# Last token block's products moved to the end, state loads moved behind the third up group, one normalization and one projection moved

## The chip, the cores and the metric

The kernel runs on one core of a Trainium2 chip. The time is the device time of one execution in microseconds, the median of several runs; before the change it is 433.28 us (three runs, 433.25 to 434.26). A profiled execution gives the trace from which the lines below come.

## What is computed

A gated linear-state layer followed by a feed-forward layer with binarized weights, each with a residual and a layer norm, on an input of 2 sequences of 4096 tokens with 256 features:

```python
u = x @ W_in + b_in
g = sigmoid(x @ W_gate + b_gate)
h_t = tanh(h_prev @ A + u_t @ Bm)
y_t = h_t @ C.T + u_t @ D.T
y_t = g_t * y_t + (1.0 - g_t) * x_t
x = layernorm(x + (ys @ W_out + b_out + x))

bw = mean(abs(w), axis=1) * sign(w)
h = gelu(einsum('bsd,hd->bsh', x, bw1) + b1)
out = einsum('bsh,dh->bsd', h, bw2) + b2
x = layernorm(x + out)
```

The state has 64 entries, the hidden layer of the feed-forward part 1024.

## The kernel before

**Scan and chunks.** Each sequence is cut into 64 segments of 64 steps that are scanned side by side. The scan runs 40 warm-up steps and then 64 steps; one step is a product on TensorE (PE) with 128 columns (`steps`, L165) and a tanh on ScalarE (ACT, L170). The tokens of four steps form a chunk: 512 tokens, four blocks (`TB`) of 128. There are 16 chunks. At the end a count (`compare`, `count`, L172 to L186) checks that the warm-up has converged; if not, a slow path (L892 and after) computes all again.

**A chunk's stages**, as methods of `Chunk`: `load_u` and `load_h` copy the chunk's inputs and states of the scan into the tile hu (L355, L359, on SyncE's queue, SP); `load_x`, `load_n` load x; `gate` (L322) with a tanh; `mix` (L383, PE, then L390 on VectorE, DVE); `mix_end` (L395, L398, DVE); `project` (L408, PE, two halves, then the sum L419 on DVE); `stats1` (L264 to L274: block statistics, their merge and a sum on DVE, the reciprocal root on GpSimd, POOL); `shift` (L279, DVE) and `norm` (L287, four ACT instructions of 128x256). Then the normalized chunk is transposed: chunks 0, 1 and 15 by `turn` on PE (L442) with copies to a high part (L450, ACT) and a low part (L452, DVE); the others by `blocks`, a DVE transpose (L461) and sixteen small copies on SP's queue (L467), split by `split_hi` (L475, ACT) and `split_lo` (L479, DVE).

The feed-forward part goes in four groups of 256 hidden features. `up(g)` makes two products tiles ps_h (L498), a gelu for each (L508, ACT) and a copy to the rounded high part hhi (L517, ACT); `low(g)` the low part hlo (L524, DVE); `down(g)` adds 16 products per half (L540) into ps_o: for each of two feature blocks and each token block one product with the high and one with the low part. After group 3 come `scale` (L556, DVE), `add` (L562), statistics and `store` (normalization and an output DMA, L577).

**Order.** It is written out by hand for all engines: each engine and queue runs its instructions in the program's order. The main loop (L792 to L869) goes over c = 0 to 14; iteration c runs up, low and down of chunk c, the end of chunk c-1 (down groups 2 and 3), the transposition of chunk c+1, and mix, projection and statistics of chunk c+2, and loads for chunk c+3 and beyond. `step()` puts in one scan step where the next is ready; `do(c + 3, "load")` puts in as many steps as chunk c+3's states need and then issues both state loads. In iterations 10 and 11 one more `step()` stands ahead of the mix (L806). In iteration 0, `down` group 0 stands ahead of `project` of chunk 2. In iteration 14 the normalization of chunk 15 stands between up groups 0 and 1 of chunk 14.

**Buffers.** PSUM has these pools: p_s (one tile, the scan), p_m with one buffer of two banks under the tag "m" (ps_y of mix, ps_z of the projection, ps_t of the transposes, and ps_p at the end), p_1 with three single banks under the tag "h" (ps_h, ps_g and others), p_2 with one buffer of two banks (ps_o). The tiles h have two buffers, hhi and hlo three, x tiles "xt" eight.

**The end.** After the loop, chunk 15's groups are run; `down(0, True)` puts its four token blocks on four different banks, two of ps_o and two of ps_p. Then `down_end` (L594) runs the products of groups 2 and 3 block by block (`products`), scales each block, adds blocks 0 to 2 on POOL and block 3 on DVE, gathers statistics, and normalizes and stores each block: blocks 0 and 1 on ACT (which needs a shift from DVE), 2 and 3 on DVE.

## Time and profile before

| | us |
|---|---|
| median of three runs | 433.28 |
| the profiled execution | 433.4 |
| its span, first to last instruction | 431.6 |
| last product on PE ends | 423.4 |
| DVE busy | 337.0 |
| ACT busy | 282.3 |
| POOL busy | 165.2 |
| state loads L359: issue to landing, minimum, median, maximum | 2.2, 2.3, 7.3 |
| x loads L347: issue to landing, minimum, median, maximum | 3.3, 3.5, 3.6 |
| x loads L104: issue to landing, minimum, median, maximum | 3.2, 6.4, 9.5 |

All times in the text are microseconds from the start of the span. The page gives busy time per engine, and busy shares in 40 slices of the span. A product on PE is recorded with its whole passage through the array, so records of back-to-back products overlap: what a product costs is the distance between two starts, 0.115 for 256 columns of L540, 0.23 for 512 columns of L498. "PEld" is the load of the stationary operand. The chain of waits goes back from the last instruction, at each step to what released it; "issue" is time in which nothing that the profile shows was waited for. In the timeline, square brackets hold the idle time ahead of an instruction and its releaser.

### The profile page before, as it was taken

To read this page: it belongs to the slowest core of one execution; us is meant where nothing else is said; L and a number is where in the kernel's file an instruction comes from. 1 tells how busy PE (TensorE), PEld (TensorE's weight loads), DVE (VectorE), ACT (ScalarE), POOL (GpSimd) and SP (SyncE) were. 2 spreads that over 40 slices of the span, in tenths; PEclk is the share of its full clock that TensorE was granted. 3 is DMA by queue.
4 is the path that set the end of the run, shared out by engine and by line. 5 is a ranking of instruction groups with operands and counts; after the bars stand their busy time and mean duration, and the time that the engine had idled before them with its cause. 6 is when DMAs were issued, how large, how long until landed. Compare 5 with 4: busy or idle time off the path is not lost.

```text
span 431.6 us, 6781 instructions
## 1 busy us (share of the span) xinstructions
PE 421.7 (98%) x2390; PEld 342.8 (79%) x2390; DVE 337.0 (78%) x571; ACT 282.3 (65%) x469; POOL 165.2 (38%) x176
## 2 busy tenths in 40 slices
PE   8999999999999999999999999999999999999992
PEld 5576767788978888887978787979797888888982
DVE  0255477995979797979798888889797979789684
ACT  3353533386586867777676767676777685859881
POOL 1000013574155554344525453544443444415513
PEclk9999999999999999999999999999999999999997
DMA  8885555000252625162515242524242232311102
GB/s 285 296 286 203 159 159 171 1 2 0 47 174 45 225 45 176 41 219 49 177 40 184 81 140 75 194 72 145 75 127 87 59 115 59 111 37 50 49 2 103
DMA packets 31047, 49.24 MB, mean 114 GB/s; under 512 B 5281, under 2 KB 19873, under 8 KB 31009
## 3 DMA queue, kind: packets, MB, share of 16 engines
q1 hardware_dynamic: 30432, 48.39, 35.5%
q8 instruction: 21, 0.34, 0.3%
q10 hardware_dynamic: 576, 0.37, 0.3%
q14 instruction: 18, 0.14, 0.1%
HBM read 29.33 MB, written 8.39 MB: 87 GB/s over the span
## 4 chain that ended last, share of the span: by engine, by line
PE 89%; DVE 4%; SPq 2%; ACT 2%; DMA 1%; issue 0%; POOL 0%; POOLq 0%; ACTq 0%; DVEq 0%
PE ps_h L498 24%; PE ps_o L540 24%; PE ps_g L322 13%; PE ps_z L408 12%; PE ps_y L383 6%; PE ps_s L165 5%; PE ps_u L138 3%; SPq L467 2%; ACT xn L287 1%; DMA w_gate<-in_W_gate 1%; DVE hlo L524 1%; PE ps_t L442 1%; DMA xlo<-xb 0%; PE ps_p L540 0%; DVE d L395 0%
## 5 line engine op out<-in xcount | busy, mean ns | idle before, releaser
L540 PE MATMUL ps_o<-sg,hhi 128*128 128x256 f32 x496 | 120.6, 284 | 0.2 <-DVE o L556 0.2
L540 PE MATMUL ps_o<-sg,hlo 128*128 128x256 f32 x496 | 117.6, 278 | 0.1
L508 ACT ACTIVATE h<-ps_h,bias_c,al 128x512 f32<-128x512 f32 x128 | 95.3, 771 | 15.0 <-PE ps_h L498 10.8
L368 POOL TENSOR_TENSOR xn<-xn,bo_r 128x256 f32<-128x256 f32 x64 | 61.1, 987 | 102.2 <-DVE sg L204 61.3
L540 PEld LDWEIGHTS ps_o<-sg,hhi 128*128 128x128 f32 x496 | 93.4, 188 | 1.6 <-DVE o L556 0.6
L540 PEld LDWEIGHTS ps_o<-sg,hlo 128*128 128x128 f32 x496 | 93.4, 188 | 1.4 <-DVE hlo L524 0.3
L498 PE MATMUL ps_h<-xhi,sg 128*128 128x512 f32 x256 | 92.8, 444 | 0.1
L524 DVE TENSOR_TENSOR hlo<-h,hhi 128x1024 fp32r<-128x1024 f32 (+1 forms) x65 | 80.9, 1263 | 4.6 <-ACT hhi L517 4.6
L498 PE MATMUL ps_h<-xlo,sg 128*128 128x512 f32 x256 | 79.7, 393 | 0.0
L517 ACT CAST hhi<-h 128x1024 fp32r<-128x1024 f32 (+1 forms) x65 | 67.4, 1039 | 2.0
L322 PE MATMUL ps_g<-xt,w_gate 128*128 128x384 f32 (+3 forms) x212 | 66.2, 425 | 0.3 <-DMA w_gate<-in_W_gate 0.3
L274 POOL TENSOR_TENSOR rs_b<-rs_b,neg_half 128x4 f32<-128x4 f32 (+1 forms) x17 | 28.2, 1659 | 98.4 <-DVE rs_b L273 93.4
L498 PEld LDWEIGHTS ps_h<-xhi,sg 128*128 128x128 f32 x256 | 46.5, 189 | 18.7 <-issue 9.6
L170 ACT ACTIVATE st<-ps_s 64x128 f32<-64x128 f32 x103 | 27.5, 267 | 45.9 <-PE ps_s L165 45.5
L498 PEld LDWEIGHTS ps_h<-xlo,sg 128*128 128x128 f32 x256 | 48.1, 188 | 10.9
L368 POOL TENSOR_TENSOR xn<-xn,b_r 128x256 f32<-128x256 f32 x64 | 55.8, 903 | 1.1 <-PE ps_t L442 1.1
L408 PE MATMUL ps_z<-w_out,tg 128*128 128x256 f32 x224 | 50.6, 379 | 0.0
L165 PEld LDWEIGHTS ps_s<-st,wab 128*128 128x128 f32 x208 | 35.6, 189 | 18.2 <-ACT st L170 9.3
L408 PEld LDWEIGHTS ps_z<-w_out,tg 128*128 128x128 f32 x224 | 41.4, 190 | 5.1
L475 ACT CAST xhi<-xlo 128x1024 fp32r<-128x1024 f32 x13 | 13.7, 1051 | 42.1 <-DVE nm_b L279 20.3
L165 PE MATMUL ps_s<-st,wab 128*128 128x128 f32 x208 | 40.4, 276 | 0.0
L322 PEld LDWEIGHTS ps_g<-xt,w_gate 128*128 128x128 f32 x212 | 33.1, 191 | 7.4 <-issue 5.3
(79 smaller groups left out, 485.2 us busy)
## 6 DMA issues: line engine op xcount, KB each, us to landing
xt<-in_xT SPq DMA_DIRECT2D x31, 512.0 KB, 4.3
xn<-in_x SPq DMA_DIRECT2D x16, 512.0 KB, 3.3
out_y<-xn SPq DMA_DIRECT2D x15, 512.0 KB, 2.6
xlo<-xb SPq DMA_DIRECT2D x208, 32.0 KB, 1.9
hu<-st SPq DMA_DIRECT2D x32, 128.0 KB, 2.3
w1t<-in_w1T SPq DMA_DIRECT2D x2, 512.0 KB, 5.5
w1n<-in_w SPq DMA_DIRECT2D x2, 512.0 KB, 6.7
w2t<-in_w2T SPq DMA_DIRECT2D x2, 512.0 KB, 6.9
```

Of the source, the lines that this page charges most:

```text
L165: nc.tensor.matmul(p_h, ab, st[:, j].rearrange("p b k -> p (b k)"), start=True, stop=True)
L170: nc.scalar.activation(h_of[:, j + 1].rearrange("p b k -> p (b k)"), p_h[TOP, :], AF.Tanh)
L274: nc.gpsimd.tensor_tensor(rs, rs, neg_half[:, cut], ALU.pow)
L322: nc.tensor.matmul(ps[:, cut], w_gate[:, m, k, :], xt_[:, k, cut], start=k == 0 and i == 0, stop=k == KD - 1, skip_group_check=True,)
L368: nc.gpsimd.tensor_tensor(r[:, i, :], r[:, i, :], row, ALU.add)
L383: nc.tensor.matmul(ps[:, m, :], cd[:, bass.ts(m, P)], self.hu, start=True, stop=True)
L408: nc.tensor.matmul(self.ps_z[:, i, :], self.y[:, k, bass.ts(i, P)], w_out[:, k, :], start=k == 0, stop=k == KD - 1,)
L498: nc.tensor.matmul(ps, sg1[:, k, bass.ts(j, P)], part[:, k, :], start=n == 0, stop=n == 2 * KD - 1,)
L508: nc.scalar.activation(to, ps.rearrange("p (a i c) -> p a i c", a=P // 32, c=32) if self.far else ps, AF.Gelu, bias=b1_c[:, j : j + 1], sc ...
L517: nc.scalar.copy(hi[:, part, :], h[:, part, :])
L524: nc.vector.tensor_sub(lo[:, i, :], h[:, i, :], hi[:, i, :].bitcast(FP))
L540: nc.tensor.matmul(ps[:, i, :], part[:, j % 2, bass.ts(tb, P)], sg2[:, j, :], start=j == 0 and part is self.h[j // 2][0] and first, stop=j ...
```

## The change

- The end: block 3 of chunk 15 gets no products in down groups 0 and 1; all its sixteen come last. Blocks 2 and 3 get banks of their own from the pool p_1 (`own_bank`). The high and low part of group 3 take buffers of the x tiles. Within `down_end` products run first over group 2 for three blocks, then over group 3 block by block; the statistics of blocks 0 and 1 stand ahead of block 3's scale on DVE; their shift moves from DVE to three small ACT instructions (`shift_alone`); block 3 is stored ahead of block 2, and the queues of the two are swapped.
- `load_u` stays where both state loads were, `load_h` moves behind up group 2 and its step; with it the rule that fills in missing steps. The two extra steps of iterations 10 and 11 are gone; in the order that comes out, two more steps run in iteration 12, behind its up groups 1 and 2.
- In iteration 14 the normalization of chunk 15 moves between the two gelus of up group 1.
- In iteration 0 the projection of chunk 2 moves ahead of down group 0.

```diff
+        def shift_alone(self, blocks):
+
+            cut = slice(blocks[0], blocks[-1] + 1)
+            self.sh = sm.tile([P, TB], FP, tag="nm", name=f"nm_{self.name}_{blocks[0]}")
+            nc.scalar.activation(self.sh[:, cut], self.mv[:, cut, 0], AF.Identity, scale=-1.0)
+            for i in blocks:
+                sh = self.sh[:, i : i + 1]
+                nc.scalar.activation(sh, sh, AF.Identity, scale=self.rs[:, i : i + 1])
...
-            hi = wk.tile([P, 2, N], FR, tag="hhi", name=f"hhi{nm}", bufs=3)
+            if apart:
+                hi = xp.tile([P, 2, N], FR, tag="xt", name=f"hhi{nm}", bufs=XTB)
+            else:
+                hi = wk.tile([P, 2, N], FR, tag="hhi", name=f"hhi{nm}", bufs=3)
...
-            lo = wk.tile([P, 2, N], FR, tag="hlo", name=f"hlo{self.nm}_{g}", bufs=3)
+            if apart:
+                lo = xp.tile([P, 2, N], FR, tag="xt", name=f"hlo{self.nm}_{g}", bufs=XTB)
+            else:
+                lo = wk.tile([P, 2, N], FR, tag="hlo", name=f"hlo{self.nm}_{g}", bufs=3)
...
-                self.banks = [((self.ps_o, other)[tb % 2], tb // 2 * 2, True) for tb in range(TB)]
+                self.banks = [(self.ps_o, 0, True), (other, 0, True), self.own_bank(2)]
+
+        def own_bank(self, tb):
+            ps = p_1.tile([P, N], FP, tag="h", name=f"ps_q{self.nm}_{tb}")
+            return ps.rearrange("p (i d) -> p i d", d=DM), 0, True
...
-                for tb in range(TB):
+                for tb in range(len(self.banks)):
                     self.down_part(2 * g + i, tb)
...
-            for tb in range(2):
-                products(tb)
-                add(tb)
-            st2.gather([0])
-            products(2)
-            add(2)
-            st2.gather([1])
-            st2.merge([0, 1])
-            st2.root([0, 1])
-            products(3)
-            add(3)
-            st2.shift([0, 1])
-            store(0, nc.scalar)
-            store(1, nc.scalar)
-            st2.gather([2, 3])
-            st2.merge([2, 3])
-            st2.root([2, 3])
-            store(2, nc.vector)
-            store(3, nc.vector)
+            for tb in range(last):
+                products(tb, range(KH // 2, KH - 2))
+            for tb in range(last):
+                products(tb, range(KH - 2, KH))
+                self.scale(range(tb, tb + 1))
+                add(tb, nc.gpsimd)
+            products(last, range(KH))
+            early, late = [0, 1], [2, last]
+            st2.gather(early)
+            st2.merge(early)
+            st2.root(early)
+            self.scale([last])
+            add(last, nc.vector)
+            st2.gather(late)
+            st2.merge(late)
+            st2.root(late)
+            st2.shift_alone(early)
+            store(0, nc.scalar, nc.sync)
+            store(1, nc.scalar, nc.scalar)
+            store(last, nc.vector, nc.sync)
+            store(2, nc.vector, nc.scalar)
...
-        if what == "load":
+        if what == "load_h":
             need = WARM + (ch[i].c + 1) * SPC
             while done < need:
                 next_steps()
-            ch[i].load_u()
             ch[i].load_h()
...
-                do(c + 1, "norm", nc.scalar)
             do(c - 1, "down", 2)
             if c > 0:
-                if c in (10, 11):
-                    step()
                 do(c + 2, "mix")
...
-            do(c + 3, "load")
+            do(c + 3, "load_u")
             do(c + 6, "load_x")
             if c > 0 and c % 2 == 0:
                 do(10 + c // 2, "load_gate_x")
-            do(c, "up", 1)
+            up = ch[c].up(1)
+            next(up)
+            if c == end - 1:
+                do(c + 1, "norm", nc.scalar)
+            next(up)
             step()
...
             step()
+            do(c + 3, "load_h")
             if far:
                 do(c + 1, "split_hi")
...
-            do(c, "down", 0)
+            if c > 0:
+                do(c, "down", 0)
             do(c + 2, "project", 0)
...
             do(c + 2, "project", 1)
+            if c == 0:
+                do(c, "down", 0)
```

More of the change, by code (lines that the diff above doesn't have):

```diff
@@ L596, in down_end, with products, add, store @@
             st2 = self.st2 = Stats(self.x1, f"b{self.nm}")
-            def products(tb):
-                for j in range(KH // 2, KH):
+            last = TB - 1
+            self.banks.append(self.own_bank(last))
+            def products(tb, blocks):
+                for j in blocks:
                     self.down_part(j, tb)
-                self.scale(range(tb, tb + 1))
-            def add(tb):
-                for _ in self.add(range(tb, tb + 1), nc.gpsimd if tb < TB - 1 else nc.vector):
+            def add(tb, engine):
+                for _ in self.add(range(tb, tb + 1), engine):
                     pass
-            def store(tb, engine):
+            def store(tb, engine, queue):
                 cut = slice(tb, tb + 1)
                 st2.apply([tb], engine)
-                queue = nc.scalar if tb % 2 else nc.sync
                 queue.dma_start(out=self.at(out, self.c)[:, cut, :], in_=self.x1[:, cut, :])
-            for tb in range(2):
-                products(tb)
-                add(tb)
-            st2.gather([0])
-            products(2)
-            add(2)
-            st2.gather([1])
-            st2.merge([0, 1])
-            st2.root([0, 1])
-            products(3)
-            add(3)
-            st2.shift([0, 1])
-            store(0, nc.scalar)
-            store(1, nc.scalar)
-            st2.gather([2, 3])
-            st2.merge([2, 3])
-            st2.root([2, 3])
-            store(2, nc.vector)
-            store(3, nc.vector)
+            for tb in range(last):
[19 more added lines that the diff above has]
+            store(2, nc.vector, nc.scalar)
             yield
@@ L693, in do @@
                 next_steps()
-            ch[i].load_u()
             ch[i].load_h()
-        elif what in ("load_n", "load_x", "load_gate_x"):
+        elif what in ("load_u", "load_n", "load_x", "load_gate_x"):
             getattr(ch[i], what)()
```

## The prediction

> **What bounds the kernel now.** I read the page's busy shares and slices first, to know which engine to count on; then the chain of waits over whole iterations, for the time of a normal one; then chain and timeline at the four places of the edit.

> ```profile
> PE 421.7 (98%) x2390; PEld 342.8 (79%) x2390; DVE 337.0 (78%) x571; ACT 282.3 (65%) x469; POOL 165.2 (38%) x176
> PE   8999999999999999999999999999999999999992
> PEclk9999999999999999999999999999999999999997
> ```

> TensorE (PE) is busy in every slice but the first and the last, at full clock. So an edit can win only where PE stands still, or in the last 8.2 us (423.4 to 431.6), where PE has nothing left to do. What moves between busy PE stretches without closing a hole wins nothing.

> The chain of waits around iteration 0 and the start of iteration 2 (start, duration, what):

> ```profile
> 92.78 0.22 PE ps_s L165 x2
> 93.00 2.03 PE ps_o L540 x16
> 95.03 3.47 PE ps_z L408 x16
> 98.52 1.23 DVE xn L419
> ...
> 121.22 1.98 ACT xn L287 x4
> 123.19 0.68 ACT h L508
> 123.87 0.04 issue
> 123.91 1.19 PE ps_h L498 x4
> ```

> Chunk 2's projection (ps_z) ends at 98.5; statistics, normalization and sixteen block copies follow from it, and through ACT's queue they delay a gelu to 123.19. A product of chunk 2's first up group needs the bank that this gelu frees. The timeline's products there start at 123.47 and 123.91, 0.44 apart instead of 0.23, and the next pair costs another 0.11: a hole of 0.32 us.

> The timeline of ACT and DVE just ahead of that projection (start, duration, engine, line):

> ```profile
> 92.26 1.00 ACT L450 CAST xhi<-ps_t 128x1024 fp32r<-128x1024 f32 x1
> ...
> 93.29 1.23 DVE L452 TENSOR_TENSOR xlo<-ps_t,xhi 128x1024 fp32r<-128x1024 f32 x1 [0.35 <-ACT xhi L450]
> ```

> Both read ps_t, chunk 1's transposes, and the second ends at 94.52. ps_t and ps_z share the one buffer of the pool tag "m", so no projection can start before 94.52. Today PE fills that time with the down products of L540.

> The chain at the end:

> ```profile
> 417.59 0.78 ACT h L508
> 418.37 0.52 ACT hhi L517
> 418.89 0.02 issue
> 418.91 1.30 DVE hlo L524 x2
> 420.21 0.04 issue
> 420.26 0.38 PE ps_o L540
> ...
> 423.63 0.21 DVE rs_b L273
> 423.84 0.07 issue
> 423.91 0.72 POOL rs_b L274
> 424.62 0.02 issue
> 424.65 0.16 DVE nm_b L279
> ```

> PE waits once more for the last low half (420.26). After the last product (end 423.38) DVE still has older work: the last block's scale starts at 423.74, and its statistics stand behind a shift that waits for POOL's root.

> **The change, part by part.**

> *Chunk 2's projection ahead of chunk 0's down group 0.* Nothing ahead of it moves, so xlo still ends at 94.52; with the 0.04 of hand-over that the chain shows elsewhere ("issue") the projection starts at 94.56. The step's two products start at 92.62 and 92.73, 0.11 apart, so PE could issue at 92.84: a hole of 1.72. A product after a wait costs 0.10 more (0.38 against 0.28 at 420.26): 1.82. In return down group 0, now later, loses its own wait for the low half that DVE ends at 92.93: 2.03 becomes 1.83, as in all later iterations. Net +1.62. Does the hole of 0.32 close? The projection ends at 94.56 + 0.10 + 3.45 = 98.11 against 98.32 by the same count (95.03's piece issues from 94.87), hardly sooner. But chunk 0's last up group, and so its gelus (99.45), cast and tanh (end 102.39), move by 1.62, and chunk 2's normalization stands behind them on ACT: 103.87 instead of 103.52. The whole chain to the gelu of 123.19 thus comes 0.35 later, PE 1.62 later; the bank is free 1.06 us ahead of need and the 0.32 is saved. **+1.30**. Behind the waiting product stand, on PE, the projection, down group 0 and up group 3; who waits for them is ACT with group 3's gelus and what follows those, counted above. Ends: +1.2 (no restart cost) and +1.6 (the 0.32 is not saved); below that nothing, since the order on ACT and DVE up to xlo is untouched. The transfers in between wait for DVE's transpose, not for a queue that this moves.

> *States fetched behind the third up group.* Two scan steps leave iterations 10 and 11 and come back in 12. Iterations, up group 3 to up group 3: 275.14 to 297.38 is 22.24, with the extra step 297.38 to 319.90 is 22.52, so a step there costs 0.28; the iteration that lacks two steps (342.41 to 364.31) takes 21.90, so there a step costs 0.17. 2 x (0.17 - 0.28) = **-0.2**; ends -0.3 and 0. On SP's queue the state fetch (128 KB) now stands behind one or two x loads of 512 KB. Its cover: in iteration 2 it would be issued at 142.19, the products that read it start at 149.23, and the two loads, issued 0.6 earlier than today, are through at about 146.4 (today 147.0 in the packet counts); 128 KB more are 0.8. Two us are left. The output store and the next load behind it on SP wait for ACT and for that store anyway. Cost 0.

> *Chunk 15's norm between two gelus.* ACT waits 0.34 for the shift at 393.76 and the two gelus (395.74) stand behind it; after, one gelu goes first, so the rest ends some 0.3 sooner. PE's only answer is at 396.59, where a bank wait stretches one gap from 0.23 to 0.30: **-0.07**; ends -0.1 and 0. The transposes that need the norm start at 397.59, the norm would end at 396.2.

> *The end.* Down groups 0 and 1 leave out block 3, so 4 of 16 products at 0.115 each fall away ahead of up group 3: it starts 0.46 sooner. The first gelu is held by ACT and the low half that ends at 416.49; it starts at 416.6, the second at 417.23 instead of 417.59, so the last low half ends at about 419.83 instead of 420.20. PE reaches it after 12 + 12 + 3 products, at 420.0: no wait, and PE ends 0.24 sooner, at 423.14, with block 3's sixteen products last. Blocks 0, 1, 2 are ready at 420.28, 420.74, 421.20. POOL adds them one after another (0.74 each, 0.10 between, 0.14 from DVE): ends 421.63, 422.47, 423.30. DVE's statistics of blocks 0 and 1 end with the root's sum at 423.18 + 0.20; block 3's scale starts 0.11 after that one's start, as today: 423.29 instead of 423.74. That is 0.45; the shift, now on ACT, frees another 0.08 (424.65 to 424.73). Everything after runs as today: last apply 426.9, last store 426.95 instead of 427.47, then the same 4.1 us. **-0.53**. The three small ACT instructions for the shift have no row; 0.27 (the 64x128 tanh) is the nearest, 0.59 (a 128x256 normalization) the upper end. From POOL's root at 424.17 two of them and two normalizations end at 425.9 or 426.5, before 426.95 either way, so ACT hides them; beyond 0.85 each the ACT-issued store would be late. Ends: -0.24 (PE's wait alone) and -0.6.

> [...] Block 3's add (L562) falls into POOL's root again. The trace has the same overlap: root 423.91 to 424.61, add 424.19 with 0.43, no longer than the 0.43 of scales from PSUM. [...]

> Sum: +1.30 - 0.20 - 0.07 - 0.53 = **+0.5**. Against the profiled execution (433.4, span 431.6) that is 433.9; this execution lay 0.12 above the median of the runs, 433.28, so I predict 433.8.

> **Rivals.**
> 1. *The projection does not wait.* For it: the edit brings it forward to feed a chain that is really late at 123.19. Against: one buffer, and a reader that ends at 94.52. Then -0.32 -0.2 -0.07 -0.53 = -1.1: 432.2.
> 2. *The end gains nothing*, because DVE and POOL, not PE, set it and their row of work is as long as before. For it: 3 adds of 0.74 are still serial; against: the scale at 423.74 stands behind early statistics that get 0.4 of lead. 434.3.
> 3. *Slower: the state fetch lands too late* behind two x loads, in the even iterations 2 to 10. From issue to need there are 7.0, 7.5, 7.8, 7.3 and 8.1 us (today's issue plus 1.2, against the products' start); it decides from a landing of 7.0 us on. Against: today's fetches land in 2.3 us by the median, 7.3 at most (0.3 us lost). At 9.5, the longest landing of any x load, PE would lose 2.5 + 2.0 + 1.7 + 2.2 + 1.4 = 9.8: 443.7.
> 4. *Slower: the hole lowers the clock.* At the end the granted clock averages 0.70 over 424 to 432, full speed until about 427.2, 3.8 us after the last product. The hole is 1.7, so I expect full clock; I give it little, without a price of its own.

> **How the numbers follow.** Forecast 0.74 (433.2 to 434.5 by the ends above); rival 1: 0.06; rival 2: 0.08; rival 3: 0.04; rival 4 and unknown waits 0.08. The range 432.7 to 434.9 takes in rival 2 and half of the unknown. A measurement can tell about 0.3%, 1.3 us, from no change (the runs shown span 1.0 us). Faster by more needs 432.0 or less: rival 1 with luck, 0.04. Slower by more needs 434.6 or more: rivals 3 and 4 and the upper tails, 0.14. Within: 0.82.

> **What would show it.** Right: PE idle for 1.7 us at about 93 with DVE's xlo as releaser; no gap at chunk 2's first up group; no wait near 420; block 3's scale 0.1 to 0.2 after the last product; iterations 10 and 11 back at 22.24. Wrong: no hole at 93 (rival 1), ps_y waiting for hu (rival 3), products twice as long after 94 (rival 4), or a new wait in ACT's queue at the end.

## The result, and the profile after

The changed kernel takes 434.86 us (median of 22 executions, 434.12 to 437.06), the kernel of before 433.93 (22 executions beside it). The ratio is 1.0024 with a 95% interval of 1.0017 to 1.0032, so the change costs +1.04 us (0.74 to 1.39; the plain difference of the two medians is 0.93). I had forecast +0.5 us and given 0.82 to a change too small to be told from none. The profiled execution took 434.5, its span is 432.7, against 433.4 and 431.6 before. One execution of `d_alone` below took 877.8 us, twice the others; its ratio leaves that one out, and why it was so long is not known.

One thing must be said of the base first. The median before, 433.28, came from three executions. Over the later comparisons it was 433.7 to 434.0, and the profiled execution to which I had added my sum (433.4) lay below that too. So of the 1.06 us between 433.8 and 434.86, 0.65 belong to the base and the rest to the sum. Below, only differences are used.

Lines of code stand lower in the changed kernel: L417 is the old L408, L461 the old L452, L488 the old L479, and L510, L520, L529, L539, L559, L575 are the old L498, L508, L517, L524, L540, L556. Three lines of the page after:

```profile
PE 421.6 (97%) x2390; PEld 343.4 (79%) x2390; DVE 339.3 (78%) x570; ACT 282.0 (65%) x472; POOL 164.1 (38%) x176
PE   8999999989999999999999999999999999999992
PEclk9999999999999999999999999999999999999998
```

PE does the same work in the same 421.6 us; the ninth slice, 86.5 to 97.4, now is an 8, and the granted clock (PEclk) stays full there, 1.00. The timeline of PE there (start, duration, what, in brackets the idle time ahead of it and its releaser):

```profile
92.55 0.38 PE L165 MATMUL ps_s<-st,wab 128*128 128x128 f32 x2
94.50 0.48 PE L417 MATMUL ps_z<-w_out,tg 128*128 128x256 f32 x1 [1.56 <-DVE xlo L461]
```

The hole is where and as long as foretold: PE waits for DVE's low half of chunk 1, which frees the one buffer "m". From the step's last start, 92.66, to the projection's first, 94.50, are 1.83 us; 0.11 is a normal distance, so 1.72 are lost.

The chain of waits at the place of the old 0.32 us hole, chunk 2's first up group:

```profile
115.45 1.89 PE ps_o L559 x16
117.33 3.45 PE ps_z L417 x16
120.79 1.84 PE ps_h L510 x8
122.63 0.22 PE ps_s L165 x2
```

No gelu is in the chain any more: that hole is closed. At the end the chain reads:

```profile
416.06 1.85 PE ps_h L510 x8
417.91 0.04 issue
417.95 1.45 ACT h L520 x2
419.40 0.52 ACT hhi L529
419.92 0.02 issue
419.94 1.30 DVE hlo L539 x2
421.25 0.04 issue
421.29 0.40 PE ps_o L559
421.69 0.02 issue
421.71 0.44 DVE o L575
```

I had foretold "no wait near 420". PE does wait for the last low half, at 421.25, and not a little later than before but 1.03 us later (the low half ended at 420.20 before, ends at 421.24 now). That is more than PE's own lag: PE is 0.80 us behind the old kernel at chunk 15's transposes (398.39 against 397.59), for it has closed a hole of 0.37 us at 378.6 by the way. DVE is 1.37 us behind in the same stretch (low part of chunk 14: 388.00 against 386.63; low part of chunk 15: 403.42 against 402.04) and stays there. Two engines carry two different delays to the end. DVE's line for chunk 14's low part, before and after:

```profile
386.63 1.23 DVE L479 TENSOR_TENSOR xlo<-xlo,xhi 128x1024 fp32r<-128x1024 f32 x1 [1.05 <-ACT xhi L475]
```
```profile
388.00 1.23 DVE L488 TENSOR_TENSOR xlo<-xlo,xhi 128x1024 fp32r<-128x1024 f32 x1 [1.59 <-ACT xhi L484]
```

### The profile page after: what moved, and what is told of

Its sections match the earlier page's. It is cut to its first block, busy times and chain, and to the rows that moved or that the text cites. A ratio compares the mean times of both kernels' runs of the same rounds, so it can differ in the third digit from the quotient of the medians.

```text
span 432.7 us, 6785 instructions
## 1 busy us (share of the span) xinstructions
PE 421.6 (97%) x2390; PEld 343.4 (79%) x2390; DVE 339.3 (78%) x570; ACT 282.0 (65%) x472; POOL 164.1 (38%) x176
## 4 chain that ended last, share of the span: by engine, by line
PE 94%; DVE 1%; ACT 1%; DMA 1%; issue 1%; POOL 0%; SPq 0%; POOLq 0%; DVEq 0%
PE ps_h L510 26%; PE ps_o L559 26%; PE ps_g L331 13%; PE ps_z L417 13%; PE ps_y L392 6%; PE ps_s L165 5%; PE ps_u L138 3%; DMA w_gate<-in_W_gate 1%; ACT h L520 1%; PE ps_t L451 0%; DVE hlo L539 0%; DVE xlo L461 0%; POOL xn L581 0%; DVE bs_b L264 0%; ACT xhi L459 0%
## 5 line engine op out<-in xcount | busy, mean ns | idle before, releaser
L559 PE MATMUL ps_o<-sg,hhi 128*128 128x256 f32 x488 | 118.7, 285 | 0.0
L559 PE MATMUL ps_o<-sg,hlo 128*128 128x256 f32 x488 | 115.5, 278 | 0.1
L520 ACT ACTIVATE h<-ps_h,bias_c,al 128x512 f32<-128x512 f32 x128 | 94.9, 770 | 16.9 <-PE ps_h L510 8.4
L559 PEld LDWEIGHTS ps_o<-sg,hlo 128*128 128x128 f32 x488 | 91.8, 188 | 1.5 <-DVE hlo L539 0.5
L559 PEld LDWEIGHTS ps_o<-sg,hhi 128*128 128x128 f32 x488 | 91.9, 188 | 1.1 <-DVE o L575 0.2
L510 PE MATMUL ps_h<-xhi,sg 128*128 128x512 f32 x256 | 92.5, 443 | 0.0
L539 DVE TENSOR_TENSOR hlo<-h,hhi 128x1024 fp32r<-128x1024 f32 (+1 forms) x65 | 81.4, 1271 | 5.2 <-ACT hhi L529 4.9
L510 PE MATMUL ps_h<-xlo,sg 128*128 128x512 f32 x256 | 79.7, 393 | 0.0
L529 ACT CAST hhi<-h 128x1024 fp32r<-128x1024 f32 (+1 forms) x65 | 67.5, 1039 | 2.0
L274 POOL TENSOR_TENSOR rs_b<-rs_b,neg_half 128x4 f32<-128x4 f32 (+1 forms) x17 | 28.2, 1658 | 99.5 <-DVE rs_b L273 94.6
L510 PEld LDWEIGHTS ps_h<-xhi,sg 128*128 128x128 f32 x256 | 46.6, 189 | 18.1 <-issue 9.6
L510 PEld LDWEIGHTS ps_h<-xlo,sg 128*128 128x128 f32 x256 | 48.1, 188 | 11.0
L377 POOL TENSOR_TENSOR xn<-xn,b_r 128x256 f32<-128x256 f32 x64 | 54.7, 884 | 1.0 <-PE ps_t L451 1.0
L417 PE MATMUL ps_z<-w_out,tg 128*128 128x256 f32 x224 | 50.7, 379 | 1.6 <-DVE xlo L461 1.6
L165 PEld LDWEIGHTS ps_s<-st,wab 128*128 128x128 f32 x208 | 35.7, 189 | 18.4 <-ACT st L170 9.3
L417 PEld LDWEIGHTS ps_z<-w_out,tg 128*128 128x128 f32 x224 | 41.4, 190 | 6.9 <-DVE xlo L461 1.8
L165 PE MATMUL ps_s<-st,wab 128*128 128x128 f32 x208 | 40.4, 276 | 0.0
```

The costliest lines, as they stand in the source:

```text
L165: nc.tensor.matmul(p_h, ab, st[:, j].rearrange("p b k -> p (b k)"), start=True, stop=True)
L274: nc.gpsimd.tensor_tensor(rs, rs, neg_half[:, cut], ALU.pow)
L377: nc.gpsimd.tensor_tensor(r[:, i, :], r[:, i, :], row, ALU.add)
L417: nc.tensor.matmul(self.ps_z[:, i, :], self.y[:, k, bass.ts(i, P)], w_out[:, k, :], start=k == 0, stop=k == KD - 1,)
L510: nc.tensor.matmul(ps, sg1[:, k, bass.ts(j, P)], part[:, k, :], start=n == 0, stop=n == 2 * KD - 1,)
L520: nc.scalar.activation(to, ps.rearrange("p (a i c) -> p a i c", a=P // 32, c=32) if self.far else ps, AF.Gelu, bias=b1_c[:, j : j + 1], sc ...
```

## The experiments

Fourteen runs, each of 5 to 12 executions; each ratio is to 15 to 29 executions of the kernel before, made beside them on the same chip. Two theories run through the expectations. "One clock" is the prediction's: what PE wins or loses adds up to the end. "Two clocks": from chunk 14's copies on, DVE and ACT carry their own delay to the last low half.

**The parts alone, and the change without its projection.** `d_alone` moves only the projection in the kernel of before, by the edit below; `without_d` takes the same edit back out of the changed kernel:

```diff
-            do(c, "down", 0)
+            if c > 0:
+                do(c, "down", 0)
             do(c + 2, "project", 0)
...
             do(c + 2, "project", 1)
+            if c == 0:
+                do(c, "down", 0)
```

> Only chunk 2's projection goes ahead of down group 0; all else as before. The one-clock theory (the prediction's: what PE loses or wins reaches the end) expects a hole of about 1.6 us at 93 on PE, no gap at chunk 2's first up group, and +1.3 us less whatever later holes of PE close: near +0.95 if the 0.365 us hole at 378.6 closes as it did with the whole change. The two-clock theory (from chunk 14's block copies on, DVE and ACT carry their own delay to the last low half, and PE's closed holes only make PE wait there) expects DVE's xlo of chunk 14 and the last low half +1.37 us, a longer PE wait at the last low half than the 0.24 of before, and a span +1.4 us.

Measured: 435.73 us, ratio 1.0037 (1.0023 to 1.0050), +1.6 us.

> The whole change but for chunk 2's projection, which stays behind down group 0. One-clock theory: -0.2 -0.07 -0.53 = -0.8 us against before. Two-clock theory: -0.2 of the fetch reaches DVE's clock, the norm's 0.07 does not, the end gives -0.77 at the last store's issue: about -0.9 there, and -0.4 in the span if the 0.5 us after the last store's issue come again.

Measured: 433.20 us, ratio 0.9981 (0.9972 to 0.9990), -0.8 us, with 4.64 us after the last store's issue again. The two add up to +0.8, near the +1.04 of both together: the projection's move is the whole loss, and without it the change is a gain. The two theories are not told apart by `d_alone`: in its profile the hole at 378.6 closed by only 0.07 us, so both expect the same.

`end_alone` takes over only the hunks of `shift_alone`, `up` and `low` with `apart`, `own_bank`, `down_tiles`, `down` and `down_end`:

```diff
-                self.banks = [((self.ps_o, other)[tb % 2], tb // 2 * 2, True) for tb in range(TB)]
+                self.banks = [(self.ps_o, 0, True), (other, 0, True), self.own_bank(2)]
```

> Only the end is changed: block 3's products whole at the end, its shift on ACT, the new order of stores. The prediction's price is -0.53 us. Read against DVE's clock, the trace of the whole change gives -0.77 us up to the issue of the last store, and +0.5 us after it. If those 0.5 us belong to the new order of stores, the span falls by only about 0.25 us here and the time from the last store's issue to the end is about 4.6 us, not 4.1; if they are chance, the span falls by about 0.75 us.

Measured: 433.05 us, ratio 0.9977 (0.9965 to 0.9988), -1.0 us, and 4.15 us from the last store's issue to the end of the span. So the end by itself is worth my 0.53 or more (the interval is 0.5 to 1.5 us), and the new order of the stores alone does not bring the 0.5 us after the last store.

`fetch_alone` and `norm_alone`:

```diff
-                if c in (10, 11):
-                    step()
...
-            do(c + 3, "load")
+            do(c + 3, "load_u")
...
             step()
+            do(c + 3, "load_h")
```

> Only the states' fetch is moved behind the third up group (two scan steps go from iterations 10 and 11 to 12). Prediction: -0.2 us: iterations 10 and 11 back at 22.24 us, iteration 12 longer by 0.35. Rival: the fetch, now behind x loads on SP's queue, is late somewhere and PE waits at ps_y: any loss of over 0.2 us. Two clocks: PE is 0.2 us sooner at chunk 14's projection, and DVE's xlo of chunk 14 by the same 0.2.

Measured: 433.58 us, ratio 0.9991 (0.9982 to 1.0000), -0.4 us. No wait at ps_y; from chunk 5's mix to chunk 14's projection PE takes 211.44 us instead of 211.63: -0.19, as predicted. In the changed kernel iterations 10 and 11 take 22.25 us again.

```diff
-                do(c + 1, "norm", nc.scalar)
             do(c - 1, "down", 2)
...
-            do(c, "up", 1)
+            up = ch[c].up(1)
+            next(up)
+            if c == end - 1:
+                do(c + 1, "norm", nc.scalar)
+            next(up)
```

> Only chunk 15's norm goes between the two gelus. Prediction: -0.07 us. Two-clock theory: ACT is some 0.4 us sooner from there to chunk 15's first gelus and PE waits less at chunk 15's transposes, but DVE's xlo of chunk 15 and with it the last low half keep their distance to DVE's xlo of chunk 14: nothing at the end.

Measured: 433.80 us, ratio 0.9993 (0.9984 to 1.0002): not to be told from nothing. From DVE's low part of chunk 14 to that of chunk 15 it takes 15.39 us, before 15.41: DVE did not profit up to there. The stretch from chunk 14's low part to the last low half, though, is 33.24 us, before 33.57; the account below comes back to it.

`without_end` is the three parts together, without the end:

> The change without its end: projection, fetch and norm. By the prediction's terms +1.30 -0.20 -0.07 = +1.03 us. By the runs so far (PE 1.40 us late by the projection, 0.2 of it won back by the fetch) +1.2 us at the last low half, and about 4.15 us from the last store's issue to the end, since without the end's extra ACT instructions ACT's last drain is not late. If the whole change's excess over my sum lies in the end, this kernel is at +1.0; if it lies in the projection, it is at +1.5 or more.

Measured: 435.09 us, ratio 1.0026 (1.0016 to 1.0035), +1.1 us. The changed kernel, with the end on top, has 1.0024: an end that alone wins 1.0 us wins nothing there. That asked for a cause.

**The late drain.** Each engine closes the kernel with instructions called drains, at which the engines wait for one another (before the change SP's is the last to end, 3.42 us after the issue of the last store, and POOL goes on at 3.45). The page leaves them out; the raw trace has them. Start after the issue of the last store, us, of ACT's last two drains, with the number of ACT's instructions (rows) in the trace:

```
kernel         ACT rows   first drain   last drain   end of span
before              574          1.52         3.66          4.15
d_alone             574          1.52         4.27          4.75
end_alone           578          1.50         3.71          4.15
after               579          3.77         4.16          4.64
without_d           579          3.77         4.16          4.64
```

The one to watch is the first of the two; "the drain" and the expectations' "last drain" mean it. POOL goes on only when it is through (in the changed kernel it ends at 3.91 and POOL goes on at 3.94). In the two kernels with 579 rows this drain runs 2.25 us later than elsewhere, and later than the stores have landed (SP is through with waiting for them at 3.5). `end_alone` ends with the same instructions, and its drain is on time; what differs is how many ACT instructions stand ahead. The padded kernel, which writes a scratch value of one element five times instead of once:

```diff
-    nc.scalar.activation(flag_f, neg_half[0:1, 0:1], AF.Gelu)
+    for _ in range(5):
+        nc.scalar.activation(flag_f, neg_half[0:1, 0:1], AF.Gelu)
```

> The whole change, with four more ACT instructions of one element at about 3 us, where ACT waits for data. In the traces of the whole change and of the change without its projection (579 ACT rows each) ACT's last drain runs 3.77 us after the last store's issue, in all others (574 to 578 rows) at 1.5 us. Theory: a block of ACT's code begins just at that drain, and four instructions more put the border ahead of the place the last branch jumps to: the drain is back at 1.5 us and the time from the last store's issue to the end falls from 4.64 to 4.15 to 4.3 us, the span by some 0.35 us. Rival: the late drain is chance or belongs to the order of the stores; then nothing changes.

Measured: 434.42 us, ratio 1.0007 (0.9999 to 1.0016); the drain at 2.04 us, the end at 4.55 (I had expected 4.15 to 4.3). Then the same with eight, beside the changed kernel as it is, and the kernel of before lengthened to 579 rows:

> The changed kernel itself, beside the padded one on one chip. Its ratio so far is 1.0024. Code-border theory: ACT's last drain again 3.77 us after the last store's issue, and never less than 4.6 us from there to the end. Chance: a drain at 1.5 us. The padded kernel of the same call must be faster by 0.2 to 0.7 us if the border is what takes the end's gain.

> The changed kernel with eight more ACT instructions of one element at about 3 us (587 ACT rows). Code-border theory: the drain at 1.5 to 2 us, the time after the last store's issue as in the kernels without the late drain, 4.15 to 4.8 us, ratio to before 1.0007 to 1.0019. Rival: the four instructions helped by something else at the start; then the drain is late again or the ratio stays at 1.0024.

> The kernel of before with five more ACT instructions of one element at about 3 us, 579 ACT rows as in the changed kernel; no other change. Code-border theory: its last drain goes from 1.5 to 3.77 us after the last store's issue and the end is never sooner than 4.6 us after that issue; the time rises by some 0.2 us. Rival (the late drain belongs to the new order of the stores): the drain stays at 1.5 us.

Measured: the changed kernel 434.88 us, ratio 1.0030 (1.0018 to 1.0042), drain at 3.84, end at 4.71; with eight more 434.40 us, 1.0014 (1.0004 to 1.0023), drain at 1.51, end at 4.12; the kernel of before with five more 434.12 us, 1.0008 (0.9998 to 1.0017), drain at 3.66 instead of 1.52, end at 4.53. Five instructions of one element at 3 us, where ACT is idle, make this drain late by 2.1 us at the end of the kernel, 430 us on: it goes with the number of ACT instructions ahead of it and not with the order of the stores. Its price in a profile is the part by which it outlasts the stores: 0.36 us in the changed kernel's first profile, 0.14 in the second, 0.31 in `without_d`, 0.28 in `before_pad5`. It is not the only thing that lengthens the end: in `without_end`, `d_alone` and `fetch_alone` the drain is on time, and the end still comes at 4.63, 4.75 and 4.80; I put that down to stores that land later (in `d_alone` the last drain is at 4.27 instead of 3.66, with the first on time).

**The two clocks.** DVE's chain in the tail has one place where it waits for ACT for 3.4 us (406.46 to 409.82 before): ACT's four normalizations of chunk 13 wait for DVE's shift, which stands behind a low half. `before_shift` moves it ahead:

```diff
+            if c == end - 1:
+                ch[c - 1].st2.shift(range(TB))
             do(c, "low", 2)
```

> The kernel of before, with chunk 13's shift on DVE ahead of chunk 14's low half of group 2. Two-clock theory: ACT's four normalizations of chunk 13 start 1.0 us sooner (after the cast that ends at 404.28 instead of at 405.30), and so does DVE's low half of chunk 15's group 0; where DVE came late to the tail, PE's wait at the last low half shrinks: -0.2 to -0.5 us at the median, but no more, since the last up group's products then hold the last gelus. In the best kernel, whose last up group starts 0.46 us sooner, the same move gave more. One-clock theory: nothing.

Measured: 433.90 us, ratio 1.0001 (0.9992 to 1.0011). I had expected 0.2 to 0.5; it is nothing. ACT's normalizations of chunk 13 do follow the cast at once (404.60), and DVE's low half comes sooner (409.13). But the last product of the last up group starts at 417.58 and the gelu that needs it at 418.02, as far apart as before (417.16 and 417.59): PE, not DVE, decides there. `best` is the change without its projection, with the same move and the four added instructions:

> The change without its projection, with the four added ACT instructions, and chunk 13's shift on DVE ahead of chunk 14's low half of group 2 instead of behind it. Two-clock theory: ACT's four normalizations of chunk 13 start about 1 us sooner, so DVE's low halves of chunk 15 do, and PE no longer waits for the last low half; with the code border this gives -0.3 to -0.7 us against the change without its projection, about -1.2 to -1.5 against before. One-clock theory: the shift changes nothing, only the code border's 0.35 us is won.

Measured: 432.07 us, ratio 0.9953 (0.9940 to 0.9966), -2.0 us, faster than both kernels of this study. Again, beside the same kernel without the move:

> The change without its projection, with four more ACT instructions of one element at about 3 us; chunk 13's shift where it was. Code-border theory: ACT's last drain at 1.5 to 2 us, and faster than the change without its projection (ratio 0.9981) by 0.2 to 0.5 us: 0.997 to 0.9977. If the border costs nothing, 0.9981 again. If nearly all of the best kernel's 2.0 us is here too, the shift has no part in it.

> The best kernel once more, beside the same without the earlier shift. Two-clock theory: the shift is worth 0.5 to 0.9 us here, though it was worth nothing in the kernel of before, since here the last up group starts 0.46 us sooner and no longer holds the last gelus: last low half 0.5 to 0.9 us sooner, no PE wait there. Rival: the first measurement was a lucky one of five runs; then the two kernels agree within 0.2 us.

Measured: without the move 433.07 us, 0.9981 (0.9970 to 0.9992); with it 432.49 us, 0.9963 (0.9949 to 0.9977). The move is worth 0.8 us by the two ratios, whose intervals overlap. In the profiles the stretch from chunk 14's low part to the last low half is 32.66 and 32.14 us with the move and 33.23 without; the span gains in the first of the two only (430.4 and 431.2 against 431.3), since the stretch ahead came out longer in the second (26.89 us against 26.03). The chain at the end of `best`:

```profile
417.97 0.46 PE ps_o L560 x4
418.43 0.45 PE ps_p L560 x4
418.88 0.45 PE ps_q L560 x4
419.33 0.47 PE ps_o L560 x4
419.80 0.02 issue
419.82 0.44 DVE o L576
```

There is no ACT and no DVE between PE's products: the low half is there in time, and PE runs through to the first scale. And without the projection the padding wins nothing that can be told (0.9981 both times).

## Why the prediction was wrong, point by point

The span falls into stretches that can be compared in all sixteen profiles (before, after and the fourteen), since each kernel has a part or does not. Each stretch begins where the one above it ends. Medians or extremes, us, with the number of profiles:

| stretch | without the part | with it | difference | predicted |
|---|---|---|---|---|
| step ahead of the projection to chunk 5's mix | 56.39 (56.09 to 56.93, 10) | 57.73 (57.69 to 57.78, 6) | +1.34 | +1.30 |
| to chunk 14's projection (fetch) | 211.63 (6) | 211.44 (10) | -0.19 | -0.20 |
| to DVE's low part of chunk 14 | 25.7 to 26.9 (16) | | chance | 0 |
| to the last low half (end or norm) | 33.35 to 33.58 (5) | 33.21 to 33.24 (9) | -0.34 | -0.37 - 0.07 |
| to the last store's issue (end) | 7.25 to 7.33 (7) | 6.80 to 6.85 (7) | -0.46 | -0.16 |
| to the end of the span (579 ACT rows) | 4.38 (4.12 to 4.80, 12) | 4.64 (4.53 to 4.71, 4) | +0.26 | 0 |

The two profiles of `best` are left out of the fourth and fifth row, since the earlier shift changes them (32.66 and 32.14, 6.93 and 6.92).

*The projection.* Right, in place and size: hole 1.72, restart 0.10 (the first product took 0.48, the others 0.38), the 0.32 us hole closed. It is the whole loss; the change would have done best to leave it out. Rival 1 (no wait) is ruled out by the hole, rival 4 (a lower clock) by the clock row (1.00 from 86.5 to 97.4).

*The state fetch.* Right. Rival 3, a late landing, did not come: no wait at ps_y.

*The norm.* Its reason was right, its price was read from one profile and is not a fixed one. The hole in chunk 14's third up group, where PE waits for a gelu that stands behind the norm on ACT, costs 0.07 us in that profile. In the five other profiles with the norm in its old place it costs 0.02 to 0.82 us, in the ten with the norm moved nothing. PE's products there in `fetch_alone`, where the next pair costs another 0.11, and in `norm_alone`:

```profile
397.10 0.74 PE L498 MATMUL ps_h<-xhi,sg 128*128 128x512 f32 x2 [0.37 <-ACT h L508]
```
```profile
396.78 0.62 PE L498 MATMUL ps_h<-xhi,sg 128*128 128x512 f32 x2
```

From chunk 14's low part to the last low half `norm_alone` takes 33.24 us and `without_end` 33.23, no more than `end_alone` (33.21). So the norm and the end win the same 0.34, and together they win it once. In time, the norm by itself can't be told from nothing.

*The end.* By itself it does what I had worked out up to the last low half: -0.34, where I had 0.37 less for the second gelu that no longer waits for PE. In `end_alone` PE does not wait for the low half; in the changed kernel it does, since DVE comes later there. Behind the low half the end wins 0.46 (6.81 against 7.27), where I had 0.16, because POOL's three adds run without the pause of 0.10 that I put between them (starts 422.28, 422.98 and 423.67), and the three small ACT instructions take 0.20, 0.30 and 0.28 beside other work. Rival 2 (the end gains nothing) is wrong for the end itself. On top of the other three parts the end does show nothing (1.0026 without it, 1.0024 with it). The stretches suggest why: the norm has already won the 0.34, and the late drain takes up to 0.36 of the rest.

*The steps that failed.* In the sum it is the last line of the end's working: "Everything after runs as today: last apply 426.9, last store 426.95 instead of 427.47, then the same 4.1 us." The time after the last store, put at no change, measured 4.64 and 4.71 us in the changed kernel's two profiles against 4.15 before: +0.49 and +0.56, as much as the whole end was to win. Of this the late drain is 0.36 and 0.14; the rest is stores that landed later (in the first profile SP is through with waiting for them at 3.49 instead of 3.36), and there the 4.1 us were at the short end of what this code shows (4.12 to 4.80 where the drain is on time). The drain is late in all four profiles with 579 ACT rows, and the three added ACT instructions, with what goes with them, brought the kernel to that number. I had asked whether they hide beside other work, and not what a longer program does to the end of it.

In the forecast it is the bound: "A measurement can tell about 0.3%, 1.3 us, from no change (the runs shown span 1.0 us)." It was drawn from three executions, and by it my own +0.5 counted as no change. With 22 executions against 22 the interval reaches some 0.3 us to either side, so +0.5 would have been told from nothing, and +1.04 is.

*The sum.* +1.34 - 0.19 - 0.34 - 0.46 + 0.26 = +0.61. Without the late drain it is +0.35, and the padded kernels measure +0.3 and +0.6. The changed kernel itself measures +1.04 and +1.3, so some 0.4 us more than its stretches explain, and their cause stays open. The two profiles before and after do differ by as much as the times, 1.1 us: they have +0.49 after the last store instead of +0.26, +0.18 in the stretch put down to chance, and +1.44 for the projection. But that stretch alone varies by 1.2 us from profile to profile, and one profile for each kernel does not tell its mean. By differences of ratios the projection costs 1.1 us (with the padding) to 2.1 us (without), so a part may lie there. That the drain costs more in the median execution than in the profiled ones is possible; it was not shown, and without the projection the padding won nothing.

*The two clocks.* Adding up what PE wins and loses was wrong in kind, though it cost little here: "no wait near 420" and the norm's fixed price came of it. The row "to the last low half" shows it: from DVE's low part of chunk 14 to the last low half it takes 33.21 to 33.24 us in nine kernels, whether PE, at chunk 15's transposes, is 0.54 us ahead of the old kernel (`without_d`) or 0.80 behind (after). Only the earlier shift made it less (32.66 and 32.14 in the two profiles of the best kernel). So the hole that PE closed at 378.6 was worth nothing.

## What to carry to other kernels

Before a producer is brought forward on an engine, look at who last reads the buffer it writes: here a reader on DVE that ended 1.7 us later was in the profile, and no gain downstream (0.32) could pay for it. Where the end of a kernel is a chain of several engines, measure each stretch of it from its own releaser; a hole closed on the busiest engine counts only if that engine is the last to arrive (here PE's 0.37 us at 378.6 won nothing). A hole's size in one profile is one sample: the norm's was 0.07 us there and up to 0.82 elsewhere. And take the base from as many executions as the comparison will have: three put it 0.65 too low.

## What the hardware showed that I had not expected

```profile
365.49 1.22 DVE L479 TENSOR_TENSOR xlo<-xlo,xhi 128x1024 fp32r<-128x1024 f32 x1
```
```profile
363.31 4.00 POOL L368 TENSOR_TENSOR xn<-xn,b_r 128x256 f32<-128x256 f32 x4
```

and in `d_alone`:

```profile
366.89 1.66 DVE L479 TENSOR_TENSOR xlo<-xlo,xhi 128x1024 fp32r<-128x1024 f32 x1
```
```profile
364.48 2.98 POOL L368 TENSOR_TENSOR xn<-xn,b_r 128x256 f32<-128x256 f32 x4
```

Same instructions, same data. Before, DVE starts 0.04 us ahead of POOL's fourth add and takes its 1.22; POOL's four adds take 4.00, the fourth alone 1.78 after 0.75 for the third. In `d_alone` POOL's fourth add began 0.17 us ahead: POOL's four take 2.98, and DVE's subtraction 1.66. Over the sixteen profiles this one instruction takes 1.22 to 1.84 us, and its excess over 1.22 is what was left of POOL's add, less about 0.13. Which of the two waits changes at a few hundredths: in `after_pad8` the starts lie 0.01 us apart, and DVE waits. Some hundredths of a microsecond upstream thus become up to 0.6 on DVE's chain. The stretch from chunk 14's projection to chunk 14's low part goes with it: its median is 25.95 us in the eight profiles where this instruction took under 1.5 us and 26.51 in the eight where it took more, a good part of the 1.2 us by which it varies. The row I had gone by, the last add (0.43 us) beside POOL's root of 128x2 (0.71), stands in the changed kernel too (0.43 beside 0.71), so the root there did not block it. Why not is not shown; it was the wrong row to generalize from.

*Code blocks.* A handful of ACT instructions at 3 us decide whether the drain runs 1.5 or 3.8 us after the last store. The theory that a block of ACT's code begins just there was my guess; no trace shows it. The trace has the loads of code as packets of 8 and 16 KB, some of them in the last 5 us of every run, and one packet of 8 KB moves with the count: it starts 0.2 us after the last store's issue with 583 rows (drain at 2.04 and 2.09) and 2.3 us ahead of it with 584 and 587 (drain at 1.51), while with 574 to 579 rows none starts within 8 us ahead of that issue or 1 us behind it. Whose code a packet holds the trace does not say.
